# A gated unit through the SiLU table, and a replanned instruction order, in a two-layer cross-attention and feed-forward kernel

## The chip, the core and the metric

The kernel runs on one core of one Trainium2 chip. A core has a matrix engine (TensorE, PE in the profile, with its weight loads listed apart as PEld), a vector engine (VectorE, DVE), an activation engine (ScalarE, ACT), a general engine (GpSimd, POOL) and an engine that here only issues transfers (SyncE, SP). Each works through its own list of instructions in order and waits on semaphores for the others. The metric is the time of one execution on the device, in microseconds (us).

## What is computed

Both layers are pre-normalised residual blocks over 8192 tokens of width 128 (128 sequences of 64), with a second tensor of the same shape as context. Cut to what matters:

```python
x = x + L0_xattn(layernorm(x), ctx, ctx)   # 16 heads of width 8, layer norms, sigmoid gate
x = x + L0_ffn(layernorm(x))
x = x + L1_xattn(layernorm(x), ctx, ctx)   # 16 heads of width 8
x = x + L1_ffn(layernorm(x))               # 128 -> 512, relu, 512 -> 128

def L0_ffn(x):                             # tlin(x, w, s) = (x @ w.T) * s, w in {-1, 0, 1}
    h = silu(tlin(x, w1_w, w1_s)) * tlin(x, w2_w, w2_s)   # 128 -> 512
    h = gelu(tlin(h, h1_w, h1_s))                         # 512 -> 512
    h = gelu(tlin(h, h2_w, h2_s))                         # 512 -> 512
    return tlin(h, w3_w, w3_s)                            # 512 -> 128

def attention(q, k, v):                    # per head
    return softmax(q @ k.T * 8**-0.5) @ v
```

The change sits in the first line of `L0_ffn`, in the way attention's normalising sums are formed, and in the order of everything.

## The kernel before, in words

The tokens are cut into 17 chunks: 15 of 512 tokens and, at both ends, one of 256. A chunk passes four stages: `attention0`, `ffn0`, `attention1`, `ffn1`. Several chunks are under way at once, each in another stage, so that the engines always have something from some chunk.

**The order is planned.** Every stage is a Python generator that yields an `Op` (engine or engines it may run on, a name, what buffers it takes and gives back) and then emits the instructions of that step. `Order.run` keeps a clock per engine. It looks at all streams that have a step to offer, works out when each could start (`start_of`, from the durations in `LENGTHS`, the buffers in `RESOURCES` and the ends of earlier steps), and emits the one with the smallest key: earliest start, then priority. The priority is the stage's own (or the step's `prio`) plus `PRIO[name]` plus a pseudo-random draw scaled by `SPREAD`, seeded by `DRAWS` for each 50 us of planned time. A step that needs another activation table than the one loaded has `SWITCH` added to its start in the key and `TABLE` (1.3) to its planned duration. Where a step may run on two or three engines, the one with the earliest end plus `BIAS` is taken. What comes out is a fixed order of instructions on each engine. On the chip nothing of this planning runs; the order and the choice of engines are all that is left of it.

**The gated unit** is `gated` (L1024 is the helper `by_parts`, which emits its matmuls and all other matmuls of `ffn0`). For each quarter k of the 512 hidden columns, PE forms two products in two banks, `pa` and `pb`. ScalarE computes tanh of `pa` times `half_s1` (L1033); SiLU follows from it as a x sigmoid(a) = (tanh(a/2) + 1) x a/2. VectorE does this in two fused operations: `(tanh + 1) * pa` (L1035) and `* half_s12 * pb` (L1036). Then `parts` splits the result into a rounded high part (L569, L571 or L573 by engine) and a low part (L1020), which the next matmuls read. The gelu steps (L1058) do the same for the 512 x 512 layers, with the table "gelu"; attention's softmax (L759) and the gate of layer 0 (L935) use the table "exp". The tanh step names no table.

**Attention** runs in halves of four sequences, 64 halves in all. `attend` forms the scores (L723), takes their maximum on VectorE (L726), turns it to rows (L742, copied by L745), forms scores less the maximum (L754) and the exponential (L759). Then there are two forms. Where `MIX[index]` is 0 (index is twice the chunk's number, plus 1 for the second layer), 64 matmuls (L776) give weighted values and sums together in two masked products. ScalarE and VectorE take them apart (L786, L787, L789, L790), VectorE takes the reciprocal (L793) and swaps partitions (L794), and GpSimd or VectorE multiplies (L837). Where `MIX[index]` is 1, `apart` uses 128 matmuls (L811) to put sums and values in place at once, and VectorE only takes the reciprocal (L821) and multiplies (L837).

**At the start** `masks` (L534 to L542) makes the head masks and masked biases on VectorE, which the first keys (L656) and queries need, `folds` (L893 to L909) makes the selection matrices and `half_s1`, `half_s12`, and `blanks` (L546 to L555) clears buffers on GpSimd. `context0` is the first step of `attention0`: it normalises the context (L600, L602, rsqrt by L588) and makes keys (L677) and values (L690).

Of the kernel before, what the change touches and what calls it, by code (L numbers as in the profile page):

```python
# [8 lines left out]
F32 = mybir.dt.float32  # L9
# [3 lines left out]
AF = mybir.ActivationFunctionType  # L13
# [3 lines left out]
P = 128  # L17
# [23 lines left out]
for _n, _w in _COLS:  # L41
# [25 lines left out]
DRAWS = [0, 752, 0, 0, 880, 0, 0, 0, 0, 670, 0, 0, 452, 631, 18, 551, 473, 276, 0, 0, 0, 266, 0, 0]  # L67
SPREAD = 0.78
MIX = [0, 1, 1, 1, 0, 1, 0, 1, 0, 1, 0, 1, 0, 1, 0, 1, 0, 1, 0, 1, 1, 0, 1, 1, 0, 0, 0, 0, 0, 0, 1, 0, 0, 0]
PRIO = {"apart": 5.27, "exp": -0.93, "f1": 4.02, "from bank": -0.06, "gained z": 3.09, "gate": -3.01, "gate exp": -1.94, "gate sums": 2.21, "gated": -9.82, "gelu": 2.8, "high": 3.08, "k": -0.62, "kx": 1.22, "low bank": -1.0, "max": -1.99, "max copied": -0.61, "o2": 1.48, "oT": -1.19, "q": 0.6, "qx": -1.5, "reciprocal": -2.05, "reciprocal apart": -0.89, "relu": 1.99, "rsqrt gate": 4.42, "scaled": -1.16, "scores": 1.96, "square": 4.06, "tanh": 0.13, "tokens": -3.66, "tokens 4": 4.71, "two masked": 0.58, "vb": -1.49, "w12": -2.09, "w3": 3.5, "weighted values": 1.91, "z": -0.47}  # L70
SWITCH = 0.23
# [7 lines left out]
BIAS = {("copied", ACT): 0.04, ("high", ACT): 0.9, ("high", POOL): 0.87, ("kx", ACT): -0.91, ("kx", DVE): -1, ("low", POOL): -0.07, ("parts", DVE): 0.61, ("parts", POOL): -0.7, ("qx", ACT): -0.09, ("qx", DVE): -1, ("relu", ACT): 1.36, ("relu", DVE): -0.06, ("scaled", ACT): -0.57, ("scaled", DVE): -0.14, ("vb", ACT): 0.11, ("vb", DVE): -0.07, ("w3", ACT): -1.0, ("w3", DVE): 1.09, ("z", ACT): 0.23, ("z", DVE): -0.4, ("z", POOL): 0.16}  # L79
# [6 lines left out]
        "scores": (1.0, 0.2), "max transpose": (0.07, 0.2), "scores less max": (1.18, 0.2),  # L86
        "weighted values": (0.93, 0.2), "apart": (1.85, 0.2), "tokens": (0.23, 0.15), "tokens 4": (0.9, 0.15), "w12": (0.95, 0.1),
# [3 lines left out]
        "bias+": 0.28, "masks": 1.2, "exact?": 0.7, "flag": 0.2, "flag out": 0.15, "rounded": 0.42, "high": 0.42,  # L91
        "low": 0.69, "low bank": 0.69, "w3": 0.75, "gate weights": 0.4, "folds": 1.95, "moments": 1.12, "z": 1.13,
        "copied": 0.69, "scaled": 0.81, "qx": 1.53, "kx": 1.53, "vb": 1.74, "max": 2.3, "parts": 0.46,
        "reciprocal": 2.23, "o2": 0.87, "reciprocal apart": 1.8, "oT": 0.4, "oT apart": 0.42, "from bank": 0.69, "gate sums": 1.0, "gate": 0.37, "gained": 1.14,
        "gained z": 1.14, "gated": 1.48, "relu": 0.75,
# [3 lines left out]
        "two masked": 0.84, "gate exp": 0.3, "tanh": 0.69, "rounded": 0.63, "high": 0.62, "w3": 0.69, "gelu": 0.7,  # L99
# [4 lines left out]
        "low": 1.28, "high": 0.75, "z": 1.5,  # L104
# [17 lines left out]
CHANGE = 0.13  # L122
# [13 lines left out]
class Op:  # L136
# [11 lines left out]
    def on(self, engine):  # L148

        self.engine, us = engine, LENGTHS[engine][self.name]  # L150
        self.us, self.lag = us if isinstance(us, tuple) else (us, 0.0)
        if self.part < 1 and self.name not in SAME:
            self.us *= self.part if engine == PE else 0.15 + 0.85 * self.part
        self.port = engine == POOL or engine == DVE and self.name in PORT
# [5 lines left out]
class Stream:  # L160
    def __init__(self, gen, prio, deps):
        self.gen, self.prio, self.deps = gen, prio, list(deps)
        self.op, self.last, self.done, self.ends, self.part = None, None, False, [], 1.0
# [15 lines left out]
class Order:  # L179
# [12 lines left out]
    def add(self, gen, prio, deps=(), part=1.0):  # L192
        s = Stream(gen, prio, deps)
        s.part = part
        self.waiting.append(s)
        return s
# [6 lines left out]
    def start_of(self, s):  # L203

        op, best = s.op, None
        got = 0.0
        for kind, n in op.get.items():
            f = self.choice(kind, n, self.clock[op.engine])
            if f is None:
                return None  # L210
            got = max([got] + [x for x, _ in f])
        for e in op.engines:
            op.on(e)
            t = max(self.clock[e], got, op.after.ready(e) if op.after else s.ready(e))
            if op.port:
                t = max(t, self.port[DVE if e == POOL else POOL])
            end = t + op.us + BIAS.get((op.name, e), 0.0)
            if best is None or end < best[0]:
                best = (end, t, e)
        op.on(best[2])  # L220
        return best[1]
# [38 lines left out]
    def advance(self, s, value=None):  # L260
        while True:
            try:
                got = s.gen.send(value)
            except StopIteration:
                s.done = True
                if s in self.streams:
                    self.streams.remove(s)
                return
            if isinstance(got, tuple):
                value = Stream(got[0], got[1], ())  # L270
                value.ends, value.part = list(s.ends), s.part
                self.streams.append(value)
                self.advance(value)
            elif isinstance(got, list):
                s.op, s.deps = None, got
                return
            else:
                s.op, s.op.draw, s.op.part = got, self.draw() * SPREAD, s.part
                return
# [15 lines left out]
    def run(self):  # L295
        while True:
            self.begin()
            best = None
            for n, s in enumerate(self.streams):
                if s.op is not None:  # L300
                    t = self.start_of(s)
                    if t is not None:
                        other = s.op.table not in (None, self.table)
                        prio = (s.prio if s.op.prio is None else s.op.prio) + PRIO.get(s.op.name, 0.0)
                        key = (t + (SWITCH if other else 0.0), prio + s.op.draw, n)
                        if best is None or key < best[0]:
                            best = (key, s, t)
# [60 lines left out]
def program(ctx, tc, x, c, cols, rows, headmask, w_a0, w_a1, w_12, w_h, w_3, w_f1, w_f2, out, odd):  # L368
# [163 lines left out]
    def masks():  # L532
        yield Op(DVE, "masks")
        nc.vector.tensor_tensor(half_mask[:, 0, 0:2], hm[:, 0, 0, :], hm[:, 0, 1, :], ALU.add)  # L534
        nc.vector.tensor_tensor(half_mask[:, 1, 0:2], hm[:, 1, 0, :], hm[:, 1, 1, :], ALU.add)
        nc.vector.tensor_tensor(half_mask[:, 0, 2:4], hm[:, 0, :, 0], hm[:, 0, :, 1], ALU.add)
        nc.vector.tensor_tensor(half_mask[:, 1, 2:4], hm[:, 1, :, 0], hm[:, 1, :, 1], ALU.add)
        nc.vector.tensor_tensor(mask, half_mask[:, 0, :], half_mask[:, 1, :], ALU.add)
        for t, i, name in (
            (bk0, 2, "L0_xattn_bk"), (bq0, 0, "L0_xattn_bq"), (bk1, 2, "L1_xattn_b_k"), (bq1, 0, "L1_xattn_b_q"),  # L540
        ):
            nc.vector.tensor_scalar(t, mask[:, i : i + 2], colv(name), None, ALU.mult)  # L542
# [19 lines left out]
    half_s1 = const.tile([P, 4], F32, tag="half_s1", name="half_s1")  # L562
    half_s12 = const.tile([P, 4], F32, tag="half_s12", name="half_s12")
# [325 lines left out]
    def folds():  # L889

        yield Op(DVE, "folds")

        nc.vector.tensor_copy(identb, ident)  # L893
        nc.vector.tensor_tensor(
            fold, ident[:, 0:64].rearrange("p (r c) -> p r c", r=2), ident[:, 64:128].rearrange("p (r c) -> p r c", r=2), ALU.add
        )
        nc.vector.tensor_tensor(fold[:, 0, :], fold[:, 0, :], fold[:, 1, :], ALU.add)
        for j in range(1, 3):
            nc.vector.tensor_tensor(
                fold[:, 0, 0:8], fold[:, 0, 0:8], fold[:, 0, 8 * j : 8 * j + 8], ALU.add  # L900
            )
        for s in range(HS):
            nc.vector.tensor_copy(
# [4 lines left out]
        nc.vector.tensor_scalar(half_s1, col[:, COL["L0_ffn_w1_s"]], 0.5, None, ALU.mult)  # L908
        nc.vector.tensor_tensor(half_s12, half_s1, col[:, COL["L0_ffn_w2_s"]], ALU.mult)  # L909


    def context0(ci, got, prio):
        if ci == 1:
            yield Op(NONE, "free", after=landed[3])
# [111 lines left out]
    def gated(k, zT, n, free, h, prio):  # L1026
        pe = yield Op(PE, "w12", get={"bank": 2, "wk": 1}, put=free)
# [3 lines left out]
        yield Op(ACT, "tanh", prio=-1)  # L1031
        th = tile_of(pe.slots["wk"][0], (P, n))
        nc.scalar.activation(th, pa, AF.Tanh, scale=half_s1[:, k : k + 1])  # L1033
        yield Op(DVE, "gated", put=pe.slots["bank"], prio=-1)
        nc.vector.scalar_tensor_tensor(th, th, 1.0, pa, ALU.add, ALU.mult)  # L1035
        nc.vector.scalar_tensor_tensor(th, th, half_s12[:, k : k + 1], pb, ALU.mult, ALU.mult)  # L1036
# [146 lines left out]
    for op, us in zip(landed, (0.0, 0.8, 2.2, 4.0, 5.0, 7.2, 12.0, 24.0, 40.0)):  # L1183
        op.end, op.lag = us, 0.0
# [20 lines left out]
    for ci in range(NCH):  # L1205
# [4 lines left out]
        a0.append(order.add(attention0(ci, pa), pa, a0[-2:-1] + arrived[ci : ci + 1] + marks[-AHEAD - 1 : -AHEAD], part))  # L1210
# [4 lines left out]
        f0.append(order.add(ffn0(ci, pf), pf, [a0[ci]], part))  # L1215
        a1.append(order.add(attention1(ci, 0), 0, [f0[ci]] + a1[-2:-1], part))
        f1.append(order.add(ffn1(ci, 4), 4, [a1[ci]] + f1[-5:-4], part))
# [52 lines left out]
```

## Time and profile before

| | |
|---|---|
| median of 3 runs | 973.07 us (973.01 to 974.03) |
| the profiled execution | 980.08 us, span 978.3 us |
| mean granted TensorE clock in it | 0.983 |
| activation table loads | 105: 52 before gelu, 44 + 8 before exp, 1 at the start; 1283 ns each |
| bytes moved | 23.3 MB, 22 GB/s over the span |

The profile is of one execution. "Busy" is the share of the span in which an engine had an instruction under way. A matmul's record holds its modelled end, so several overlap. The groups of instructions read: line, engine, operation, output and inputs, count | busy us in all, mean ns of one | idle time of the engine just before them, and what ended it. A list of waits reads: engine and line that waited, the line that released it: us in total, times, the longest in us. A timeline reads: start in us, duration in us, engine, line, operation.

Transfers weigh little, as the share of the 16 DMA engines' span by queue shows:

```profile
q1 hardware_dynamic: 35312, 20.93, 7.1%
q8 instruction: 116, 1.90, 0.8%
```

The columns are packets, megabytes and share.

### The profile page before, as it was taken

How to read it: one execution, taken by the hardware profiler on the slowest of the kernel's cores; microseconds unless marked ns; L12 is line 12 of the kernel's file. 1: busy time of each engine (PE TensorE's matmuls, PEld its weight loads, DVE VectorE, ACT ScalarE, POOL GpSimd, SP SyncE). 2: the span in 40 equal slices, each digit the busy share in tenths (PEclk: the TensorE clock that was granted, in tenths of full speed). 3: DMA queues.
4: the chain of work that ended last, by engine and by line, in shares of the span. 5: the costliest groups of instructions: out<-in, count | busy, mean ns of one | idle time of the engine just before them, and what ended most of it. 6: DMA issues, size and time to landing. Idle time of an engine off the chain costs nothing.

```text
span 978.3 us, 34107 instructions
## 1 busy us (share of the span) xinstructions
PE 922.2 (94%) x14619; PEld 726.5 (74%) x14619; DVE 835.5 (85%) x2017; ACT 667.9 (68%) x983; POOL 591.1 (60%) x1049
## 2 busy tenths in 40 slices
PE   7788899999989888999999999999999999999997
PEld 6676677867777676877777777787777777778876
DVE  7889899889987678989998989698998889887984
ACT  6466669766778455787778687768777678647440
POOL 6465658564585634867467568467967766432422
PEclk9998899999989899999999999999999999999999
DMA  8000001001000010101000000110010002000001
GB/s 279 3 24 12 14 22 35 7 12 35 14 23 2 12 35 8 40 3 35 3 13 3 3 3 2 45 45 3 2 45 3 1 3 60 3 12 13 12 24 41
DMA packets 35743, 23.32 MB, mean 24 GB/s; under 512 B 1536, under 2 KB 34304, under 8 KB 35328
## 3 DMA queue, kind: packets, MB, share of 16 engines
q1 hardware_dynamic: 35312, 20.93, 7.1%
q8 instruction: 116, 1.90, 0.8%
q14 instruction: 43, 0.35, 0.1%
q10 hardware_dynamic: 272, 0.13, 0.0%
HBM read 16.86 MB, written 4.19 MB: 22 GB/s over the span
## 4 chain that ended last, share of the span: by engine, by line
PE 46%; DVE 6%; POOL 2%; ACT 1%; issue 1%; DVEq 0%; POOLq 0%; ACTq 0%
PE banks L1024 18%; PE banks L865 6%; PE banks L1142 4%; PE banks L754 4%; PE banks L723 3%; PE banks L811 3%; PE banks L641 2%; PE banks L776 2%; PE banks L665 1%; PE banks L677 1%; PE banks L690 1%; POOL wk L631 1%; DVE nmax L726 1%; ACT e L759 1%; DVE wk L631 1%
## 5 line engine op out<-in xcount | busy, mean ns | idle before, releaser
L1024 PE MATMUL banks<-hl,wh 128*128 128x512 f32 (+1 forms) x1088 | 284.1, 402 | 5.0 <-DVE nmax L726 2.5
L1020 POOL TENSOR_TENSOR hl<-wk,hl 128x512 fp32r<-128x512 f32 (+1 forms) x168 | 205.5, 1228 | 90.5 <-ACT hl L569 77.5
L1024 PEld LDWEIGHTS banks<-hl,wh 128*128 128x128 f32 x1088 | 189.5, 190 | 53.3 <-issue 10.7
L726 DVE TENSOR_REDUCE nmax<-banks 128x32 f32<-128x2048 f32 x64 | 146.0, 2282 | 18.0 <-PE banks L723 13.2
L759 ACT ACTIVATE e<-banks 128x2048 f32<-128x2048 f32 x64 | 120.3, 1879 | 17.8 <-PE banks L754 15.2
L1058 ACT ACTIVATE wk<-banks,col 128x512 f32<-128x512 f32 (+1 forms) x136 | 88.0, 662 | 51.3 <-PE banks L1024 39.2
L588 POOL TENSOR_TENSOR nr<-nv,neg_half 128x4 f32<-128x4 f32 (+1 forms) x102 | 100.5, 986 | 8.5
L569 ACT CAST hl<-wk 128x512 fp32r<-128x512 f32 (+1 forms) x146 | 85.7, 595 | 29.1 <-DVE wk L1036 27.2
L723 PEld LDWEIGHTS banks<-kx,qx 32*128 32x128 f32 x2048 | 64.1, 188 | 24.0 <-issue 7.1
L723 PE MATMUL banks<-kx,qx 32*128 32x128 f32 x2048 | 76.4, 285 | 5.6 <-DVE qx L658 2.5
L1024 PE MATMUL banks<-zh,w 128*128 128x512 f32 (+1 forms) x272 | 70.1, 397 | 3.9 <-DVE zh L1081 1.8
L754 PE MATMUL banks<-qx,kx 32*128 32x128 f32 x2048 | 72.8, 280 | 0.0
L1058 ACT ACT_TABLE_LOAD x52 | 66.7, 1283 | 7.7 <-PE banks L1024 4.3
L738 POOL TENSOR_TENSOR nmax<-nmax 128x32 f32<-128x32 f32 x128 | 33.2, 259 | 57.0 <-DVE nmax L726 47.8
L865 PEld LDWEIGHTS banks<-wf,h 128*128 128x128 f32 x512 | 61.4, 194 | 3.6 <-issue 2.7
L754 PEld LDWEIGHTS banks<-qx,kx 32*128 32x128 f32 x2048 | 63.9, 190 | 0.0
L1142 PE MATMUL banks<-wk,wf 128*128 128x512 f32 (+1 forms) x136 | 63.8, 580 | 0.1
L865 PE MATMUL banks<-wf,h 128*128 128x128 f32 x512 | 63.9, 279 | 0.0
L793 DVE RECIPROCAL su<-su 128x256 f32<-128x256 f32 x35 | 61.0, 1743 | 0.0
L759 ACT ACT_TABLE_LOAD x44 | 56.5, 1283 | 5.2 <-DVE x L1110 2.6
L1024 PEld LDWEIGHTS banks<-zh,w 128*128 128x128 f32 x272 | 46.7, 188 | 17.5 <-DVE zh L1081 2.0
L821 DVE RECIPROCAL rec<-banks 128x256 f32<-128x256 f32 x29 | 50.7, 1750 | 9.8 <-PE banks L811 9.7
(145 smaller groups left out, 1954.8 us busy)
## 6 DMA issues: line engine op xcount, KB each, us to landing
c<-in_c_dram SPq DMA_DIRECT2D x30, 256.0 KB, 3.1
x<-in_x_dram SPq DMA_DIRECT2D x15, 256.0 KB, 3.4
out_dram<-x SPq DMA_DIRECT2D x15, 256.0 KB, 2.4
h<-in_w_h_dram SPq DMA_DIRECT2D x2, 1024.0 KB, 9.8
x<-in_w_dram SPq DMA_DIRECT2D x3, 256.0 KB, 6.7
c<-in_c_dram SPq DMA_DIRECT2D x4, 128.0 KB, 2.5
wa<-in_w_a_dram SPq DMA_DIRECT2D x2, 256.0 KB, 5.0
wf<-in_w_f_dram SPq DMA_DIRECT2D x2, 256.0 KB, 6.8
```

The lines of the kernel that those rows point to most:

```text
L569: nc.scalar.copy(out, src)
L588: nc.gpsimd.tensor_tensor(rs, ve, neg_half[:, 0:ng], ALU.pow)
L723: nc.tensor.matmul(sc[:, g, s, :], qs[h, s, :], ks[h, s, :], start=True, stop=True)
L726: nc.vector.tensor_reduce(nm[:, :, 0, :], sc.rearrange("p g s (j k) -> p g (s j) k", j=2), AX.X, ALU.max, negate=True,)
L754: nc.tensor.matmul(sT[:, g, s, :], lhs, rhs, start=(n == 0 and s == 0), stop=(n == 1), skip_group_check=True)
L759: nc.scalar.activation(e.rearrange("p g s i q -> p g (s i q)"), sT.rearrange("p g s c -> p g (s c)"), AF.Exp, scale=SCALE,)
L793: nc.vector.reciprocal(su, su)
L865: nc.tensor.matmul(ps[:, g, :], lhs(g), w, start=(n == 0), stop=(n == len(blocks) - 1),)
L1020: by.tensor_tensor(hl[:, 1], x, hl[:, 0], ALU.subtract)
L1024: nc.tensor.matmul(ps, w, hl[:, j], start=start and j == 0, stop=stop and j == PARTS - 1)
L1058: nc.scalar.activation(g, ps, AF.Gelu, scale=colv(("L0_ffn_h1_s", "L0_ffn_h2_s")[l], o))
L1142: nc.tensor.matmul(ps, wf1[:, k * P : (k + 1) * P], zT, start=True, stop=True)
```

## The change

Five things are changed.

1. `gated` uses the activation function SiLU itself, with the table "silu" and the scale `w1_s`, and one fused operation on VectorE in place of two. The bank of the first product is given back after ScalarE's step instead of after VectorE's. Quarters 1 to 3 get priorities of their own.
2. `half_s1` and `half_s12` go.
3. `masks` and `folds` may run on VectorE or GpSimd.
4. `MIX` has 12 ones of 34 in place of 15.
5. The planner gets a nudge per chunk and stage, an addition to the key for a change of PE tiling (`TURN`, 0), an addition for VectorE in the first 21 us (`EARLY`), other durations, other expected landing times of the first loads, and new values of `DRAWS`, `SPREAD`, `PRIO`, `SWITCH` and `BIAS`.

```diff
-MIX = [0, 1, 1, 1, 0, 1, 0, 1, 0, 1, 0, 1, 0, 1, 0, 1, 0, 1, 0, 1, 1, 0, 1, 1, 0, 0, 0, 0, 0, 0, 1, 0, 0, 0]
+MIX = [1, 1, 0, 0, 1, 1, 0, 0, 1, 1, 1, 1, 0, 0, 0, 1, 0, 0, 1, 0, 0, 0, 0, 0, 1, 0, 1, 0, 0, 0, 0, 0, 0, 0]
-SWITCH = 0.23
+SWITCH = 0.17
+TURN = 0.0
+EARLY = 0.15
+UNTIL = 21.0
...
-        "gained z": 1.14, "gated": 1.48, "relu": 0.75,
+        "gained z": 1.14, "gated": 0.76, "relu": 0.75,
...
-            self.us *= self.part if engine == PE else 0.15 + 0.85 * self.part
+            self.us *= self.part + (1 - self.part) * FIXED[engine]
...
-            end = t + op.us + BIAS.get((op.name, e), 0.0)
+            end = t + op.us + BIAS.get((op.name, e), 0.0) + (EARLY if e == DVE and t < UNTIL else 0.0)
...
-                        prio = (s.prio if s.op.prio is None else s.op.prio) + PRIO.get(s.op.name, 0.0)
-                        key = (t + (SWITCH if other else 0.0), prio + s.op.draw, n)
+                        prio = (s.prio if s.op.prio is None else s.op.prio) + PRIO.get(s.op.name, 0.0) + s.nudge
+                        turn = s.op.engine == PE and TILING.get(s.op.name, 0) != self.tiling
+                        key = (t + (SWITCH if other else TURN if turn else 0.0), prio + s.op.draw, n)
...
     def masks():
-        yield Op(DVE, "masks")
-        nc.vector.tensor_tensor(half_mask[:, 0, 0:2], hm[:, 0, 0, :], hm[:, 0, 1, :], ALU.add)
+        op = yield Op((DVE, POOL), "masks")
+        by = nc.gpsimd if op.engine == POOL else nc.vector
+        by.tensor_tensor(half_mask[:, 0, 0:2], hm[:, 0, 0, :], hm[:, 0, 1, :], ALU.add)
...
     def folds():
-        yield Op(DVE, "folds")
+        op = yield Op((DVE, POOL), "folds")
+        by = nc.gpsimd if op.engine == POOL else nc.vector
...
-        nc.vector.tensor_scalar(half_s1, col[:, COL["L0_ffn_w1_s"]], 0.5, None, ALU.mult)
-        nc.vector.tensor_tensor(half_s12, half_s1, col[:, COL["L0_ffn_w2_s"]], ALU.mult)
...
-        pe = yield Op(PE, "w12", get={"bank": 2, "wk": 1}, put=free)
+        pe = yield Op(PE, "w12", get={"bank": 2, "wk": 1}, put=free, prio=-2 if k else None)
...
-        yield Op(ACT, "tanh", prio=-1)
+        yield Op(ACT, "silu", put=pe.slots["bank"][:1], table="silu", prio=-3 if k else None)
         th = tile_of(pe.slots["wk"][0], (P, n))
-        nc.scalar.activation(th, pa, AF.Tanh, scale=half_s1[:, k : k + 1])
-        yield Op(DVE, "gated", put=pe.slots["bank"], prio=-1)
-        nc.vector.scalar_tensor_tensor(th, th, 1.0, pa, ALU.add, ALU.mult)
-        nc.vector.scalar_tensor_tensor(th, th, half_s12[:, k : k + 1], pb, ALU.mult, ALU.mult)
+        nc.scalar.activation(th, pa, AF.Silu, scale=colv("L0_ffn_w1_s", k))
+        yield Op(DVE, "gated", put=pe.slots["bank"][1:], prio=-1)
+        nc.vector.scalar_tensor_tensor(th, th, colv("L0_ffn_w2_s", k), pb, ALU.mult, ALU.mult)
...
-    for op, us in zip(landed, (0.0, 0.8, 2.2, 4.0, 5.0, 7.2, 12.0, 24.0, 40.0)):
+    for op, us in zip(landed, (3.3, 3.6, 4.2, 6.0, 7.0, 9.0, 13.0, 25.0, 40.0)):
...
-        f0.append(order.add(ffn0(ci, pf), pf, [a0[ci]], part))
+        f0.append(order.add(ffn0(ci, pf), pf, [a0[ci]], part, NUDGE["f0"][ci]))
```

`NUDGE` holds 17 numbers for each of the four stages, most between -5 and 5.

## The prediction

> **What bounds the kernel now.** I read the page's busy times first, then the slices, then the waits of each engine, then the groups of the lines that the change touches, and last the timeline around one gated unit.
>
> ```profile
> span 978.3 us, 34107 instructions
> PE 922.2 (94%) x14619; PEld 726.5 (74%) x14619; DVE 835.5 (85%) x2017; ACT 667.9 (68%) x983; POOL 591.1 (60%) x1049
> PE   7788899999989888999999999999999999999997
> DVE  7889899889987678989998989698998889887984
> ```
>
> PE looks full, and DVE is second. But the PE figure is a union of modelled records. On the chain of waits, runs of eight L1024 matmuls of 512 columns take 1.84 to 2.05 us where they follow each other, that is 0.23 each, while the group's mean is 0.40. The 1496 matmuls of that line (88 a chunk; 2 of the 17 chunks are half wide) need about 1320 x 0.232 + 176 x 0.116 = 327 us, and their records sum to 284.1 + 70.1 + 33.4 = 388. So some 60 us of L1024's "busy" is spreading and pipelining, beside the 56 us in which PE is idle. PE is nearly the bound, with perhaps 100 us of slack that other engines cause. Who causes it:
>
> ```profile
> PE banks L865 <- DVE nmax L726: 5.2, 2, 2.8
> PE banks L641 <- ACT e L759: 4.9, 2, 2.6
> PE banks L776 <- ACT e L759: 3.6, 2, 2.5
> PE banks L1024 <- DVE nmax L726: 3.2, 2, 2.5
> PE banks L723 <- DVE qx L658: 2.5, 2, 1.6
> ```
>
> These are PE's longest waits, in us, times, longest. Adding the whole list by releaser gives some 22 us for DVE and 23 us for ACT: small waits, spread over many lines, with no single stall to remove. DVE's part is work that queues on DVE (the maximum L726, 2.28 us each), so less DVE work anywhere brings those releases forward. In the middle, 150 to 950 us, PE is busy 774.9 and DVE 690.5 of 800.
>
> **The gated unit.** The lines touched:
>
> ```profile
> L1036 DVE SCALAR_TENSOR_TENSOR wk<-wk,half_s,banks 128x512 f32<-128x512 f32 (+1 forms) x68 | 48.7, 716 | 6.5
> L1035 DVE SCALAR_TENSOR_TENSOR wk<-wk,banks 128x512 f32<-128x512 f32 (+1 forms) x68 | 43.8, 645 | 5.4 <-ACT wk L1033 5.4
> L1033 ACT ACTIVATE wk<-banks,half_s 128x512 f32<-128x512 f32 (+1 forms) x68 | 42.9, 661 | 14.0 <-PE banks L1024 13.5 <-issue 0.3
> ```
>
> L1035 goes: 68 x 0.645 = 43.8 us less on DVE, and the two half_s operations at the start (0.16 us each) with it. L1036 keeps its form, 48.7 us. The SiLU activation has the shape, source and pointer scale of L1033; gelu L1058 at the same shape takes 0.687 as L1033 does, so I cost it at the same 42.9. The bank of the first product is given back after ScalarE instead of after both DVE operations, at least 1.4 us earlier. Of the unit's output the timeline shows this:
>
> ```profile
> 194.65 0.68 DVE L1035 SCALAR_TENSOR_TENSOR wk<-wk,banks 128x512 f32<-128x512 f32 x1
> 194.76 0.63 ACT L569 CAST hl<-wk 128x512 fp32r<-128x512 f32 x1 [0.24 <-DVE wk L1036]
> 195.43 0.75 DVE L1036 SCALAR_TENSOR_TENSOR wk<-wk,half_s,banks 128x512 f32<-128x512 f32 x1
> 196.09 0.68 DVE L1035 SCALAR_TENSOR_TENSOR wk<-wk,banks 128x512 f32<-128x512 f32 x1
> 196.21 0.62 ACT L569 CAST hl<-wk 128x512 fp32r<-128x512 f32 x1 [0.82 <-DVE wk L1036]
> 196.88 0.75 DVE L1036 SCALAR_TENSOR_TENSOR wk<-wk,half_s,banks 128x512 f32<-128x512 f32 x1
> ```
>
> The rounding to the high part (L569) follows at DVE's pace of 1.45 us per quarter; with one operation the pace is 0.75. In the list of waits "ACT hl L569 <- DVE wk L1036" is 27.2 us over 34 times; this should fall below half. PE itself waits for L1035 and L1036 only some 6 us in all.
>
> **What SiLU adds: table loads.** Before, loads stand only ahead of gelu and exp; no tanh brings one, whichever table is in.
>
> ```profile
> L1058 ACT ACT_TABLE_LOAD x52 | 66.7, 1283 | 7.7 <-PE banks L1024 4.3 <-issue 1.7 <-DVE wk L623 0.8
> L759 ACT ACT_TABLE_LOAD x44 | 56.5, 1283 | 5.2 <-DVE x L1110 2.6 <-DVE x L1137 1.4 <-DVE h L1147 0.4
> ```
>
> The edit names a third table, so each visit to it costs one load, and a second one if it interrupts a run of exp or gelu. Along ScalarE's timeline the tanh stand in 20 stretches: 14 right before a load (one load more) and 6 inside a run (two more). If SiLU fell in the same places that is 14 + 12 = 26 loads, 26 x 1.283 = 33.4 us. The least is one per chunk, 17, 21.8 us; the most is two per activation, 136, 174 us. The priority of -3 for quarters 1 to 3 holds the four together, so I take 26. What they cover is ScalarE's 310 us of idle time; without that cover each load delays what is queued behind it on ScalarE, the exp and the copy of the transposed maxima (L745) above all, for which PE waits. The ACT-released idle of PE, 23 us for 668 us of ACT work, would price 33 us at 1 us; full exposure is 33 us. I take 4 us, because the list of waits has ACT idle in most places.
>
> The Trainium skill speaks against this edit: "ScalarE: Activation LUTs", in "What ACT_TABLE_LOAD costs", has 1283 ns for the load and some 1380 ns of drain, 2.66 us per switch, and its section on table sets asks for grouping by set. In the trace the load at 461.35 starts as L648 ends and the exp starts at 462.64, so no drain shows there; by the page 26 switches would hold ScalarE 69 us, not 33.
>
> **Where MIX moves work.** The list has 15 ones before and 12 after; those of chunk 0 count one half, the others two. So 29 halves (the count of L821) become 22, and 7 go from the summed form (L811, 128 matmuls) to the masked form (L776, 64).
>
> ```profile
> 473.46 2.05 PE banks L1024 x8
> 849.53 1.93 PE banks L776 x128
> 556.08 1.92 PE banks L811 x128
> ```
>
> On the chain 128 of either take 1.92 us, so each half saves 0.96 us of PE, 6.7 us in all (by the busy sums, 97.1 / 29 less 40.0 / 35, it would be 15). DVE pays: L789, L790, L793, L794 sum to 3.14 us against L821 and L837's 2.17, so 7 x 0.97 = 6.8. ACT pays L786 and L787, 0.94, so 6.6. POOL pays up to 7 x 0.73 = 5.1, and has 40% idle.
>
> **Small edits.** Masks may go to POOL: nine instructions, 6.68 to 8.74 us on DVE, and the first keys (L656 at 9.05) wait for them as for PE. On POOL, at 0.2 us for the small rows there, it is 1.8 us behind 1.4 us fills (L555): between 2 us gained and 2 lost at the start. The folds (4.86 to 6.48) are needed first at 17.04 by L742; 0 to 1.6 us of DVE. I take 0 for both. Priorities, nudges, seeds and the cost table emit no instruction; they permute the five queues, the waits on SP's loads and stores among them. Their worth can't be read from the trace; PE's 56 idle us bound a gain, and a bad order could cost as much. I take 0, with 10 us either way for the range.
>
> **The sum.** PE 922.2 - 6.7 = 915.5. DVE 835.5 - 43.8 - 0.3 + 6.8 = 798.2, a relief of 37.3. ACT 667.9 + 33.4 + 6.6 = 708, 72%. If PE alone bound, the gain would be 6.7; if DVE alone, 37.3. With PE busy at 97% in the middle by records but with hidden slack, I take half of the difference: 6.7 + 15.3 = 22, less 4 for the loads: 18 us. The profiled execution, 980.08 us with a span of 978.3, would become 962 and 960. It lies 7 us above the median of the runs, 973.07, so the prediction is 955.
>
> **Rivals.**
> - *Relief on both engines (the forecast), 65%.* 938 to 970. For it: DVE at 44 to 46 of 50 us in most stretches, and the two longest PE waits by DVE are queueing behind L726.
> - *PE alone binds, 13%.* DVE's freed time only becomes idle: 973.1 - 6.7 + 2 of loads = 968. For it: the slices of PE read 9 from 40% on. Against: matmuls at 0.40 mean where 0.23 is possible.
> - *Table loads become the bound of the path (slower), 17%.* SiLU arrives while exp is running, two loads per visit. If the 68 activations come in pairs inside runs, 34 visits, that is 68 loads, 87 us; ACT rises to 762, 78%, and a third of the loads on the path, 29 us, against the 22 gained gives 980. It decides from 17 exposed loads (22 / 1.283), one per chunk. For it: exp is followed at once by PE waits (L776, L641 wait 12 us for L759), and the unit now has a load between product and activation. Against: 14 of 20 stretches already stand at a change of table.
> - *The relief doesn't reach the end, 5%.* The gains are given back in the new order, 971 to 975.
>
> **Chances and range.** About 0.2%, 1.9 us, is what a measurement of this kernel can tell from no change. Faster: the first two, 0.78; same: the last, 0.05; slower 0.17. The low end is the whole DVE relief, 973.1 - 37.3 = 936; the high end takes in the weaker half of the slower rival, 979, leaving some 0.09 above it and 0.07 below. The forecast's own range is 938 to 970.
>
> **What would show it.** Right: no second gated operation, 68 fewer DVE instructions in it; DVE busy near 798, PE near 915; 120 to 140 table loads with the ones at SiLU some 17 to 26; "hl L569 <- DVE" below 14 us. Wrong: SiLU loads above 35 or exp loads well above 52 with PE waiting on L759 above 25 us; DVE idle grown by all of 37 us with the span unchanged; or new PE waits on lines that the change doesn't touch, which would be the order.

## The result, and the profile after

The changed kernel is no faster, and by its first timing 0.6% slower, where 18 us less were forecast. Beside the kernel before, on the same chip, it took 978.75 us at the median (976.92 to 982.86, 7 runs) against 973.86 (973.01 to 974.52, 7 runs): ratio 1.0055, 95% interval 1.0039 to 1.0072. In a later sitting it was 978.27 against 977.00: ratio 1.0013, interval 0.9994 to 1.0031. The median of the kernel before itself lay between 974 and 978 us from sitting to sitting, so everything below is compared by ratios to the kernel before beside it (the ranges in us of the expectations start from about 973 to 975 for it, where they give no ratio). The profiled execution took 978.75 us.

The page after, its first lines and the slices:

```profile
span 976.9 us, 33164 instructions
PE 917.4 (94%) x14195; PEld 723.0 (74%) x14195; DVE 797.6 (82%) x1970; ACT 698.7 (72%) x1042; POOL 571.6 (59%) x1007
PE   8788889999999998999999799998999999999997
DVE  7899788887987986897889688897879887796574
```

The work moved as it was summed: DVE 797.6 us busy (798.2 forecast), PE 917.4 (915.5), ACT 698.7 (708). The gated unit and its loads, by groups (line, engine, operation, tiles, count | busy us, mean ns | idle before):

```profile
L1038 DVE SCALAR_TENSOR_TENSOR wk<-wk,col,banks 128x512 f32<-128x512 f32 (+1 forms) x68 | 45.6, 708 | 5.7 <-ACT wk L1036 5.0 <-POOL hl L1023 0.6
L1036 ACT ACTIVATE wk<-banks,col 128x512 f32<-128x512 f32 (+1 forms) x68 | 42.3, 662 | 8.0 <-PE banks L1027 7.3
L1036 ACT ACT_TABLE_LOAD x17 | 21.8, 1283 | 1.6 <-PE banks L1027 1.4
```

One operation per quarter is left on DVE, SiLU costs what tanh did, and there are 17 loads before SiLU, one per chunk; all loads together are 123, against 105. So 38 us of DVE work and 5 us of PE work went, and the span did not follow. PE's longest waits in the changed kernel (engine and line that waited, releaser: us, times, longest):

```profile
PE banks L646 <- ACT e L764: 6.5, 3, 2.6
PE banks L1027 <- DVE nmax L731: 5.4, 4, 2.5
PE banks L1027 <- ACT e L764: 5.2, 3, 2.1
PE banks L781 <- ACT e L764: 5.0, 3, 3.0
PE banks L759 <- DVE nmax L731: 2.8, 2, 2.6
PE banks L1076 <- ACT e L764: 2.5, 1, 2.5
```

Before, PE's idle time ended at the exponential for about 14 us; now it does for 24 us, mostly in pieces of 2 to 3 us. L781 reads what the exponential writes. L646 and L1076 are transposes of the context and of normalised tokens, and L1027 are feed-forward matmuls: none of these three does. (A matmul may also have to wait because it writes into a bank that the exponential reads; which bank each one writes comes below.) That is the thread that the experiments pulled.

### The profile page after: what moved, and what is told of

The parts are those of the page before. It is cut to its first block, busy times and chain, and to the rows that moved or that the text cites. A ratio compares the mean times of both kernels' runs of the same rounds, so it can differ in the third digit from the quotient of the medians.

```text
span 976.9 us, 33164 instructions
## 1 busy us (share of the span) xinstructions
PE 917.4 (94%) x14195; PEld 723.0 (74%) x14195; DVE 797.6 (82%) x1970; ACT 698.7 (72%) x1042; POOL 571.6 (59%) x1007
## 4 chain that ended last, share of the span: by engine, by line
PE 75%; DVE 11%; ACT 9%; POOL 2%; issue 2%; DMA 1%; SPq 0%; ACTq 0%; DVEq 0%; POOLq 0%
PE banks L1027 29%; PE banks L870 8%; PE banks L759 7%; PE banks L728 6%; PE banks L1144 5%; PE banks L781 4%; PE banks L816 3%; PE banks L646 3%; ACT e L764 3%; PE banks L682 3%; PE banks L670 3%; DVE nmax L731 2%; PE banks L695 2%; ACT L764 1%; DVE qx L663 1%
## 5 line engine op out<-in xcount | busy, mean ns | idle before, releaser
L1027 PE MATMUL banks<-hl,wh 128*128 128x512 f32 (+1 forms) x1088 | 284.5, 402 | 5.7 <-ACT e L764 4.0
L1027 PEld LDWEIGHTS banks<-hl,wh 128*128 128x128 f32 x1088 | 189.3, 190 | 53.6 <-issue 13.8
L1023 POOL TENSOR_TENSOR hl<-wk,hl 128x512 fp32r<-128x512 f32 (+1 forms) x145 | 176.2, 1223 | 49.3 <-ACT hl L574 36.5
L576 POOL CAST hl<-wk 128x512 fp32r<-128x512 f32 (+1 forms) x80 | 50.2, 627 | 88.1 <-ACT wk L1060 73.5
L1027 PE MATMUL banks<-zh,w 128*128 128x512 f32 (+1 forms) x272 | 70.2, 398 | 6.6 <-DVE nmax L731 5.4
L798 DVE RECIPROCAL su<-su 128x256 f32<-128x256 f32 x42 | 73.2, 1742 | 0.0
L1144 PE MATMUL banks<-wk,wf 128*128 128x512 f32 (+1 forms) x136 | 65.9, 595 | 0.2 <-DVE av L795 0.2
L1027 PEld LDWEIGHTS banks<-zh,w 128*128 128x128 f32 x272 | 47.9, 188 | 20.0 <-DVE nmax L731 7.0
L592 POOL TENSOR_SCALAR nv<-mv 128x4 f32<-128x4 f32 (+1 forms) x68 | 13.8, 203 | 80.6 <-DVE mv L607 71.8
```

The costliest lines, as they stand in the source:

```text
L576: nc.gpsimd.tensor_copy(out, src)
L798: nc.vector.reciprocal(su, su)
L1023: by.tensor_tensor(hl[:, 1], x, hl[:, 0], ALU.subtract)
L1027: nc.tensor.matmul(ps, w, hl[:, j], start=start and j == 0, stop=stop and j == PARTS - 1)
L1144: nc.tensor.matmul(ps, wf1[:, k * P : (k + 1) * P], zT, start=True, stop=True)
```

## The experiments

**Which term of the sum failed?** The planner emits a fixed order, so the unit can be swapped under an order that is kept: the planner is told the old steps and durations, and only the emitted instructions change. Four kernels, on one chip: the old order with the new unit; the old order with the second fused operation alone; the new order without SiLU's loads; the new order with a second operation put back.

Old order, new unit:

```diff
-        nc.scalar.activation(th, pa, AF.Tanh, scale=half_s1[:, k : k + 1])
+        nc.scalar.activation(th, pa, AF.Silu, scale=colv("L0_ffn_w1_s", k))
...
-        nc.vector.scalar_tensor_tensor(th, th, 1.0, pa, ALU.add, ALU.mult)
-        nc.vector.scalar_tensor_tensor(th, th, half_s12[:, k : k + 1], pb, ALU.mult, ALU.mult)
+        nc.vector.scalar_tensor_tensor(th, th, colv("L0_ffn_w2_s", k), pb, ALU.mult, ALU.mult)
```

> The order, the engines and MIX of the kernel before, unchanged; only what the gated unit emits is the new kernel's: SiLU with its table, and one fused operation on VectorE. So 68 VectorE operations (43.8 us) go and some 26 to 28 table loads come. Theory 'order' (the work is lighter, and the new order of instructions is worse by more than that): 1 to 2% faster than before, 955 to 966. Theory 'loads' (the table loads stand on the path): 972 to 985. Theory 'PE binds' (less VectorE work is worth nothing, whatever the order): 970 to 977.

Measured: 983.89 us, ratio 1.0053 (1.0032 to 1.0075), where "loads" had it and not "order". The loads rose by 26, from 105 to 131, as counted in the forecast.

Old order, tanh kept, one operation less:

```diff
-        nc.vector.scalar_tensor_tensor(th, th, 1.0, pa, ALU.add, ALU.mult)
```

> As the run before in order, but the activation stays tanh, so that no table load is added; the first of the two fused operations is left out (the unit's value is then not SiLU's). 'Order': 953 to 964, a little below the run with SiLU. 'Loads': 953 to 964 as well, with the run with SiLU 15 us or more above it. 'PE binds': 970 to 974.

Measured: 968.58 us, ratio 0.9902 (0.9875 to 0.9929). So in the old order 40 us less DVE work gave 10 us, and the 26 loads took 15.

New order, tanh in place of SiLU:

```diff
-        nc.scalar.activation(th, pa, AF.Silu, scale=colv("L0_ffn_w1_s", k))
+        nc.scalar.activation(th, pa, AF.Tanh, scale=colv("L0_ffn_w1_s", k))
```

> The new kernel with its order, and the function tanh in place of SiLU (so the unit's value is not SiLU's): about 18 table loads fewer, nothing else. 'Order': 974 to 979, the loads being mostly covered. 'Loads': 955 to 965. 'PE binds': 976 to 979.

Measured: 978.84 us, ratio 1.0012 (0.9993 to 1.0030), with 103 loads in place of 123. In the new order the loads cost between nothing and 4 us.

New order, a second operation put back:

```diff
+        nc.vector.scalar_tensor_tensor(th, pb, 0.0, th, ALU.mult, ALU.add)
         nc.vector.scalar_tensor_tensor(th, th, colv("L0_ffn_w2_s", k), pb, ALU.mult, ALU.mult)
```

> The new kernel with its order, and a second fused operation of the same shape put back on VectorE ahead of the first (it adds zero times the second product): 68 x 0.7 = 47 us more VectorE work. 'Order': 985 to 1005, since the order has no slack for it. 'Loads': 980 to 990. 'PE binds': 977 to 982, no change.

Measured: 1012.52 us, ratio 1.0360 (1.0330 to 1.0390). The new order needs the relief: DVE busy rose by 42 us and the time by 30 to 34 (1.0360 less 1.0013 to 1.0055).

For the new kernel the theory "loads" fell with the third run and "PE binds" with the second and fourth; in the old order the loads do cost. What stays is the order, with `MIX` and the moves to GpSimd in it. The second and third kernels make it plain: neither has a SiLU load, their DVE is busy 795.9 and 797.5 us, their PE 916.0 and 915.5, and still they differ by 1.1%.

**Is the new order just a bad draw?** The changed kernel again, and three kernels with other seeds (`DRAWS`), whose orders no search has picked.

> The new kernel once more, beside the kernel before and the next three on one chip. Both theories below expect the ratio of its first timing, 1.004 to 1.007; above the run with tanh in the new order (1.001) by 2 to 5 us if the 18 loads cost that.

Measured: ratio 1.0013 (0.9994 to 1.0031).

```diff
-DRAWS = [490, 0, 49, 712, 0, 884, 192, 56, 0, 0, 814, 0, 164, 643, 0, 765, 898, 0, 931, 0, 628, 0, 251, 117]
+DRAWS = [497, 0, 56, 719, 0, 891, 199, 63, 0, 0, 821, 0, 171, 650, 0, 772, 905, 0, 938, 0, 635, 0, 258, 124]
```

> The new kernel with 7 added to every seed of DRAWS that is not 0: the same work, the same MIX and rules, another order that no search has picked. The planner's own clocks end at 961 for it, at 932 for the new kernel and at 957 for the kernel before. Theory 'fitted to the planner' (the longer search gained on the planner's clocks what the chip does not give): 980 to 1000, that is 1.00 to 1.02 of the new kernel, far less than the 3% the planner puts between them. Theory 'the new order is a bad draw' (any other order of the same rules is better): 955 to 972.

Measured: 995.17 us, ratio 1.0168 (1.0136 to 1.0199).

> The same with 1 added; the planner's clocks end at 981. 'Fitted to the planner': 985 to 1015. 'A bad draw': 960 to 978.

Measured: 1025.43 us, ratio 1.0492 (1.0451 to 1.0534), worse than either theory had it.

> The kernel before with 6 added to every seed of DRAWS that is not 0: old work, old MIX, an order that no search has picked; the planner's clocks end at 971 (957 for the kernel before). 'Fitted to the planner': 980 to 1000, no better than the new kernel's unpicked orders by more than 1%. Theory 'MIX or the new rules are worse in themselves': 10 us or more below the new kernel's unpicked orders.

Measured: 996.92 us, ratio 1.0195 (1.0163 to 1.0227).

So the new order is no bad draw: the three orders that nobody picked cost 2 to 5% on the chip. But the planner thought the new order 25 us better than the old (its clocks end at 932 and 957), and the chip gave none of it.

**Where does the chip fall behind the plan?** Each maximum's start on the chip, less its planned start, along the planned time, in us:

```
before:   269:+5  320:+11  348:+19  516:+18  720:+16  925:+16
after:    289:+3  348:+7   383:+16  508:+18  543:+24  600:+27  683:+29  810:+34  903:+40
```

The plan is kept almost exactly for long stretches and lost in jumps. The jumps of before lie between 269 and 348, those of after near 300, 350 to 383, 513 to 543, 640, 780 and 870. I looked for what the plan has at those times. A half of attention takes four banks, and `FOURS` lets the planner take neighbours (0 to 3, 4 to 7 and so on) or every second bank (0, 2, 4, 6 or 1, 3, 5, 7). Groups of every second bank are planned at 194, 307, 317, 324, 329 and 345 us before, 6 of 128, and at 98, 99, 298, 354, 359, 365, 522, 527, 633, 784, 862 and 867 after, 12 of 128. They stand at the jumps. The early ones left jumps too, which were made up again: at 98 and 99 of the changed kernel PE waited 2.6 us and the lag rose from 1 to 5 us, at 194 of before it rose by 2. Only a rise of 2 us after, between 582 and 600, has no such group.

The timeline of the changed kernel at the group planned at 522 (start us, us, engine, line, operation, idle before):

```profile
540.69 0.66 PE L646 MATMUL banks<-ident,c 128*128 128x128 f32 x4
541.87 1.88 ACT L764 ACTIVATE e<-banks 128x2048 f32<-128x2048 f32 x1
543.78 0.69 DVE L578 COPY wk<-banks 128x512 f32<-128x512 f32 x1 [2.22 <-ACT e L764]
543.89 0.63 PE L1076 MATMUL banks<-ident,wk 128*128 128x128 f32 x4 [2.54 <-ACT e L764]
```

The exponential reads banks 1, 3, 5, 7 here. By the plan the first transpose (L646) is in bank 4 and the second (L1076) goes to bank 2, which VectorE had given back; neither has to do with the exponential. Yet the second transpose and the copy out of bank 4 both wait until it ends. A single instruction over every second bank spans the banks between, and it is ordered against them as well. The order is in the program's semaphores: as built from the kernel, the transpose into bank 2 and the copy out of bank 4 wait for the count that this exponential gives on ScalarE's semaphore, and the copy for nothing else. The program of the changed kernel holds such a wait of PE, on a bank between, at each of its 12 groups, and that of the kernel before at each of its 6. So nothing here shows the banks themselves to be slow or blocked. The planner knows nothing of this wait.

The stalls can then cost more than their own length, by the clock. The same stretch in windows of 4 us (window us: length, busy us of PE, PEld, DVE, ACT and POOL with counts, granted clock, DMA share, GB/s):

```profile
540.00:544.00 4.00, 1.46 (x33) 1.12 (x29) 1.78 (x10) 3.16 (x2) 2.19 (x5) 1.00 0.22 66
544.00:548.00 4.00, 4.00 (x52) 2.90 (x54) 3.62 (x9) 1.55 (x2) 0.00 (x0) 1.00 0.01 4
548.00:552.00 4.00, 1.08 (x24) 0.72 (x16) 2.53 (x11) 3.55 (x3) 2.84 (x4) 1.00 0.00 0
552.00:556.00 4.00, 3.91 (x73) 3.47 (x74) 0.00 (x0) 0.40 (x2) 3.62 (x8) 0.58 0.01 4
```

PE is busy 1.46 and 1.08 us of two of these windows, and after the second stall its granted clock falls to 0.58 for the next. The Trainium skill ("TensorE: Matmul & The Clock Gate", "HAM oscillation") describes the gate and names gaps of more than about 3.4 us as what closes it; here a gap of 3.00 us was enough, with one of 2.54 a little before it. The gap of 2.54 us alone was not: the window after it has a clock of 1.00.

**The test: split the instructions, keep the order.** Where the banks are every second one, the maximum and the exponential are issued per bank (the cut shows the exponential's part; the maximum's is alike). Nothing else changes, neither plan nor order.

```diff
+    def pieces(slots):
+        b = sorted(i for _, i in slots)
+        return [slice(0, 4)] if b[1] - b[0] == 1 else [slice(g, g + 1) for g in range(4)]
...
+        for gs in pieces(pe.slots["sc"]):
+            nc.scalar.activation(
+                e[:, gs].rearrange("p g s i q -> p g (s i q)"),
+                sT[:, gs].rearrange("p g s c -> p g (s c)"),
```

> The new kernel, same plan and order. Where the four score banks of a half are every second one (0, 2, 4, 6 or 1, 3, 5, 7), the maximum and the exponential are issued as four instructions, one per bank, in place of one over all four. Theory 'spanned banks' (an access to every second bank is ordered against the banks between as well, the planner knows nothing of these waits, and the new order has 12 such groups where the old one has 6): the waits go, 945 to 962, although the split itself adds some 10 us of ScalarE and VectorE work. Theory 'the planner's durations are off, stalls fall anywhere': no gain, 976 to 985.

Measured: 944.34 us against 974.42, ratio 0.9684 (0.9658 to 0.9709).

> The same split in the kernel before, its order kept: 6 such groups, five of them planned between 307 and 345 us, where its trace falls 13 us behind the plan. 'Spanned banks': 958 to 969, so that the new kernel with the split is 0.98 to 0.99 of it. 'Durations off': 973 to 980.

Measured: 962.53 us, ratio 0.9869 (0.9839 to 0.9899).

> Old order, SiLU and one operation (1.005 of before) with the split. 'Spanned banks': 966 to 976, the same 8 to 14 us below its form without the split as the kernel before has. 'Durations off': 980 to 986.

Measured: 967.01 us, ratio 0.9907 (0.9883 to 0.9931).

> The unpicked order of the new kernel (995 us, 1.017 of before; 13 such groups) with the split. 'Spanned banks': 962 to 980, near what the planner's clocks say (961) plus the 5 us by which every run starts late. 'Durations off': 994 to 1003.

Measured: 962.42 us, ratio 0.9873 (0.9843 to 0.9904), some 29 us below its form without the split (1.0168) and 1 us above the planner's clocks.

"Spanned banks" held in all four (the first came out just below its range), and the new kernel with the split beats both kernels. In the split programs the copy and the transposes named above wait for the exponential no longer, and PE waits for a piece only where it needs that bank or its values. Not separated is what comes of giving the four banks back one by one. The same place in the changed kernel with the split:

```profile
525.53 0.66 PE L650 MATMUL banks<-ident,c 128*128 128x128 f32 x4
525.62 2.07 ACT L770 ACTIVATE e<-banks 128x512 f32<-128x512 f32 x4 [0.25 <-PE banks L764]
526.02 0.60 PE L1082 MATMUL banks<-ident,wk 128*128 128x128 f32 x4
526.31 0.65 DVE L582 COPY wk<-banks 128x512 f32<-128x512 f32 x1
```

The transpose follows the other at once and the copy runs beside the exponential. The four pieces took 2.07 us where one instruction took 1.88. And the page of that kernel:

```profile
span 942.5 us, 33199 instructions
PE 903.3 (96%) x14195; PEld 715.1 (76%) x14195; DVE 797.1 (85%) x1976; ACT 700.0 (74%) x1072; POOL 572.0 (61%) x1007
PEclk9999999999999999999999999999999999999999
```

The busy times of DVE and ACT are those of the changed kernel, 797.1 and 700.0, in 34 us less, and PE's is 14 us less; the mean granted clock is 0.997, where it was 0.986. How much of the 34 us is the clock was not measured apart.

**Which instruction carries it, and what each term is worth without the waits.** Four more, all with their order kept.

> The new kernel with the exponential alone split by bank where the banks are every second one; the maximum stays one instruction. Of the 12 groups 10 are an exponential's and 2 a maximum's. If the exponential's access carries the waits: 944 to 950, within 0.5% of the run with both split (0.968 of before). If the maximum's does: 965 to 978.

Measured: 951.45 us, ratio 0.9730 (0.9699 to 0.9760). The exponential's ten groups carry most of it, 28 to 32 us of 32 to 36; the two maxima, left whole, still cost about 4.5 us (0.9730 less 0.9684), just outside the expected times.

> The new order with the split, the function tanh in place of SiLU (the unit's value is not SiLU's): 17 SiLU loads and a return fewer, 23 us of ScalarE work. My forecast's term for the loads was 4 us: 940, 0.964 of before. If they are covered: 943 to 945, 0.967 to 0.969. If they stand on the path: 925 to 932.

Measured: 943.75 us, ratio 0.9653 (0.9624 to 0.9682): SiLU's loads cost some 3 us, at the edge of what can be told. Loads fell by 20, to 103.

> The new order with the split, and the second fused operation put back on VectorE (adds zero times the second product; 42 to 47 us more VectorE work). Without the split it cost 30 us. If VectorE bounds the new order: 970 to 985, 0.995 to 1.01 of before. If PE alone bound it: 945 to 950.

Measured: 977.68 us, ratio 1.0010 (0.9990 to 1.0030): 43 us of DVE work put back cost about 32 us.

> The old order with the split, tanh and one operation in place of two (the unit's value is not SiLU's), no added load. Without the split this gave 10 us. With it the relief alone should give 10 to 15: 947 to 953, 0.972 to 0.977 of before, so that the run with SiLU in the same order (0.991) lies 14 us or more above it by its 26 loads.

Measured: 955.43 us, ratio 0.9765 (0.9734 to 0.9797): in the old order the relief gives 10 us; the run with SiLU in that order (0.9907) lies 14 us above, by its 26 loads. The time is 2 us above the expected ones, the ratio inside.

## Why the prediction was wrong

| kernel | ratio to before | without the spanned banks |
|---|---|---|
| before | 1 | 0.9869 |
| old order, one operation | 0.9902 | 0.9765 |
| old order, SiLU unit | 1.0053 | 0.9907 |
| new kernel | 1.0055, 1.0013 | 0.9684 |
| new order, no SiLU loads | 1.0012 | 0.9653 |
| new order, two operations | 1.0360 | 1.0010 |

- **The step that failed** is the one on the small edits: that priorities, nudges and seeds "permute the five queues" and "I take 0", with 10 us either way. The new order takes every second bank for 12 groups of four in place of 6. Those waits cost the new kernel about 34 us (1.0013 to 1.0055, less 0.9684) and the kernel before about 13 (1 less 0.9869). The difference, some 20 us, ate the gain of 18. This part is shown by the kernels with the split. What else the new order does was not nothing either, as the sum shows below.
- **Behind it stands a misreading of the profile of before.** The prediction took the list of PE's waits as "small waits, spread over many lines, with no single stall to remove". Three of its five rows are wholly or in part this one mechanism: both waits of L641, and one wait of 2.45 us in each of the two rows that end at the maximum L726. All of these are at groups of every second bank, in banks between, and none is left in the kernel before with the split. (L776 reads what the exponential writes.) A transpose of the context that waits 2.2 us for an exponential, as the row here shows, has no data from it; asking why would have led to the banks.

```profile
317.38 0.77 PE L641 MATMUL banks<-ident,c 128*128 128x128 f32 x4 [2.23 <-ACT e L759]
```

- **The sum came out right, but not its terms.** With the waits gone from both kernels, the new one is 0.9684 / 0.9869 = 0.981 of the old, 18 us of 962.5: the 18 us of the forecast. In part this is luck. With the old order kept, the new unit does not gain the 11 us that the sum gives it (15.3 for the relief less 4 for the loads); it costs 4 (0.9907 less 0.9869: relief 10, loads 14). Another 22 us (0.9907 less 0.9684) come with the new order and what is planned into it, where the sum has 6.7 for `MIX` and 0 for the order.
- **The loads:** 26 counted, if SiLU fell where the tanh stood; in the old order it was 26. In the new order the planner, which knows their price, held SiLU to one visit a chunk, 17, the stated least. The 4 us were allowed for 26 loads; the new kernel has 18 more than before, and the 20 that go with tanh in its order measured about 3. In the order that didn't plan for them 26 took 14 to 15 us of 33. That is more than the third that the slower rival put on the path, but without its 68 loads.
- **The DVE relief:** "half of the difference" stands between two measured values. It is worth 10 us of 41 when an order planned for the heavier work is kept, and 32 of 43 in an order planned without it (measured by putting the work back). This suggests that a relief of an engine is realised mostly by planning anew; no run changes the plan for this alone.
- **The rivals:** by its two ratios the changed kernel would take 974 to 978 us where the forecast has 955. "The relief doesn't reach the end", 971 to 975, is nearest in its reason: it gives the gains back "in the new order", though it doesn't say by what. The slower rival had 980, but by table loads, and the new order without SiLU's loads is at 1.0012. "PE alone binds" fell with the operation put back.
- **Confirmed:** 123 loads (120 to 140), "hl on ACT waits for DVE" 3.2 us (below 14), DVE and PE busy within 2 us. The check "new PE waits on lines that the change doesn't touch, which would be the order" is what came, and the prediction had it as a sign of being wrong.
- **Not tried apart:** MIX, the masks and folds, and the priorities. Their effect is in the ratio of the new kernel to the old, with the rest. Nor was a planner tried that may take neighbouring banks only.
- **How far the cause is shown:** one instruction over every second bank brings waits on the banks between, as semaphores in the program, and four over one bank each do not. Why the building of the program places them, by the first and last address of the access or otherwise, stays open.

## What to carry to other kernels

When the order of a kernel is planned by a model, compare the plan with the trace along its time: where the trace falls behind in jumps, there is a wait that the model doesn't know, and a longer search can find orders that run into it more often, as here 12 times for 6. Ask of each wait on the path whether the waiter needs anything of the releaser; a wait without a reason may be one that can be removed, as here in four orders. And an access with gaps may be ordered as if it had none: look at the semaphores, and issue it in pieces, or place the pieces side by side (the second was not tried here).

## What the runs showed that I had not expected

- One instruction over every second bank cost some 2 to 3 us on average (34 us for 12, 13 us for 6), while issuing it in four cost 0.2 us for the exponential (2.07 against 1.88).
- The granted clock of TensorE fell to 0.58 over 4 us after a gap of 3.00 us, and stayed at 1.00 after one of 2.54; with the split its mean rose from 0.986 to 0.997.
- Table loads cost very different amounts by the order around them: 26 took 14 us in an order that had not planned for them, 20 took about 3 us in one that had.
